# A graph network's layer 0: the node phase one block later, and reciprocal square roots on VectorE

## The chip, the cores and the metric

The kernel runs on one core of one Trainium2 chip. The metric is the device time of one execution in microseconds (us); five executions of the kernel before lie between 12327.4 and 12343.48 us, with a median of 12336.05 us. The engines are TensorE (PE in the profile, its weight loads PEld), VectorE (DVE), ScalarE (ACT), GpSimd (POOL) and SyncE (SP). DMAs are issued from the queues of SP, ACT and POOL.

## What is computed

Four graph layers run over 12500 nodes with 64 features and 212500 edges (200000 and a loop at each node); each is followed by a residual sum and a layer norm. The change touches only the first, an attention layer with 4 heads of 16 features:

```python
h = (x @ W).reshape(n, HEADS, CH)
a_src = jnp.einsum('nhc,hc->nh', h, att_src)
a_dst = jnp.einsum('nhc,hc->nh', h, att_dst)
e = jax.nn.leaky_relu(a_src[src] + a_dst[dst], NEG_SLOPE)
m = jax.ops.segment_max(e, dst, num_segments=n)
e = jnp.exp(e - m[dst])
s = jax.ops.segment_sum(e, dst, num_segments=n)
msg = h[src] * (e / (s[dst] + 1e-16))[:, :, None]
out = jax.ops.segment_sum(msg, dst, num_segments=n).reshape(n, 64) + bias
y = x + out
layer0 = (y - mean(y)) / jnp.sqrt(var(y) + 1e-5) * gamma + beta
x = _layernorm(x + layer0)
```

The next layer is a graph convolution whose edge weights are `rsqrt(deg[src]) * rsqrt(deg[dst])`; its first dense product is made at the end of layer 0's node phase. So a group of nodes needs three reciprocal square roots: one in each of two layer norms, and one of the degree.

## The kernel before

The nodes are cut into `NQ` = 128 blocks of `QB` = 98. The edges of a block lie in a tile of 128 partitions by `NJ` = 16 columns, padded. A tile of source rows, `hg`, is fetched for each block from a table in DRAM (`g0_d`), already sorted by receiving block; sums over the edges of a block are matrix products with one-hot matrices. `G` = 4 blocks are a group, of which there are 32.

Layer 0 is the stretch between about 1790 and 4025 us of the profiled execution. Its loop over blocks `d` (from L1710 on) does for each `d`:

- **Fetch** of block d+3 (L1488): one DMA from SP for `hg` (L1494) and two indirect DMAs from POOL (L1496). There are nine buffers of `hg`.
- **Place** of block d (L1585): VectorE makes the one-hot tiles `rh` (L1589), `h` (the program's `h32`, L1594, in two halves) and their product with the source scores `rv` (L1598, two halves); TensorE multiplies them into `prank` (L1603), which holds each edge's score by node and rank, and from which `largest` takes the largest score of each node. ScalarE turns `h` into `hot` (L1596), stored for the later layers. Six indirect DMAs of POOL for edge attributes (L959) follow.
- **Attend** of block d-4, which belongs to the group before (L1635): VectorE makes `ot` (L1637), TensorE multiplies it with the group's `a3` (receiver's score and maximum, in three bf16 parts) into `pd` (L1640), VectorE sums that into `ad` (L1643) and makes `z`; ScalarE takes the exponential (L1651); VectorE makes `msg` (L1652). ScalarE turns `hot` back to f32 (`o32`, L1530), and TensorE adds up `pacc` (L1532).
- After a group's fourth attend, **node0** (L1656): `xsum` out of `pacc` (L1661), two layer norms, the degree's root, a dense product (`turned4` L1390 and L1392, `dense` L1398, `tnew` L1683), and the **gather** for the next layer: `tnew` is split in three bf16 parts (L919 to L922), 42 products for each of the four blocks go to `pgat` (L931) in two halves, ScalarE copies each half to `hb` (L932) and issues the DMAs to `g_d` (L933, L934). `pgat` and `hb` have two buffers each.
- After a group's fourth place, `largest` (L1607) on VectorE and ScalarE: out of `prank` come `cnt`, `mk`, the maximum `adm`, `a3` and `pself`.

`inv_sqrt` (L1401) makes a root on ScalarE (`Sqrt`), a reciprocal and one Newton step on VectorE. ScalarE loads its function table whenever it changes between `Exp` (L1651) and `Sqrt` (L1404); those loads have the lines of the activations that need them.

SP and POOL execute in the order of the program text. On VectorE, TensorE and ScalarE a scheduler sets the order when the kernel is built, from priorities that follow the text; each engine then executes that order strictly. SP's one-hot tiles `oh` for the gather (L1511) have six buffers: the loads of a group's third and fourth one wait until the gather of the group before has used its first and second, and what stands behind them on SP (`hg`, `db` of L1706, `t0`, `x0`) waits with them.

Of the kernel before, what the change touches and what calls it, by code (L numbers as in the profile page):

```python
# [10 lines left out]
I32 = mybir.dt.int32  # L11
AF = mybir.ActivationFunctionType
OP = mybir.AluOpType
# [828 lines left out]
NQ = 128  # L842
# [7 lines left out]
G = 4  # L850
# [15 lines left out]
def tile_gnn_resnorm_d4(ctx: ExitStack, tc: tile.TileContext, a: dict, out: bass.AP):  # L866
    nc = tc.nc
    v, sca, pe, pool, sp = nc.vector, nc.scalar, nc.tensor, nc.gpsimd, nc.sync
# [453 lines left out]
    def network():  # L1322
        with ExitStack() as s0:
# [49 lines left out]
            def nt(name, w=D, bufs=2):  # L1373
                return nw.tile([QB, G, w], F32, name=name, bufs=bufs)

            def wide(t):
                return t[:QB, None, :].to_broadcast([QB, G, t.shape[-1]])

            def group(tab, g):
                return rows(tab)[:, G * g:G * g + G, :]  # L1380

            def state(tab, g, name, w=D):
                t = nt(name, w)
                sp.dma_start(t, group(tab, g))
                return t
# [15 lines left out]
            def inv_sqrt(val, shape, name):  # L1401
                sd = nw.tile(shape, F32, name=name + "_s")
                r = nw.tile(shape, F32, name=name + "_r")
                sca.activation(sd, val, AF.Sqrt)  # L1404
                v.reciprocal(r, sd)
                v.tensor_mul(sd, r, r)
                v.tensor_mul(sd, sd, val)
                v.tensor_scalar(sd, sd, -0.5, 1.5, op0=OP.mult, op1=OP.add)
                v.tensor_mul(r, r, sd)
                return r  # L1410

            def layernorm(y, dst, gamma=None, beta=None):
                s = nw.tile([QB, G], F32, name="ln_sum")
                v.tensor_reduce(out=s, in_=y, axis=AX.X, op=OP.add)
                v.tensor_scalar(s, s, -1.0 / D, None, op0=OP.mult)
                v.tensor_tensor(y, y, s[:, :, None].to_broadcast([QB, G, D]), op=OP.add)
                sq = nt("ln_sq", bufs=1)
                v.tensor_mul(sq, y, y)
                va = nw.tile([QB, G], F32, name="ln_var")
                v.tensor_reduce(out=va, in_=sq, axis=AX.X, op=OP.add)  # L1420
                v.tensor_scalar(va, va, 1.0 / D, LN_EPS, op0=OP.mult, op1=OP.add)  # L1421
                r = inv_sqrt(va, [QB, G], "ln")
                rb = r[:, :, None].to_broadcast([QB, G, D])
                if gamma is None:
                    v.tensor_tensor(dst, y, rb, op=OP.mult)
                else:
                    v.tensor_tensor(y, y, rb, op=OP.mult)
                    v.tensor_tensor(y, y, wide(gamma), op=OP.mult)
                    v.tensor_tensor(dst, y, wide(beta), op=OP.add)
# [4 lines left out]
            def heads(t):  # L1434
                return t.rearrange("p b (h c) -> p b h c", h=H)
# [52 lines left out]
            def fetch(d, w, gd, tab, parts=False):  # L1488
                if parts:
                    full = wk.tile([P, 3, NJ, w], F32, name="hg", bufs=hgbufs)  # L1490
                    hg = full[:, 0]
                else:
                    full = hg = wk.tile([P, NJ, w], F32, name="hg", bufs=hgbufs)
                sp.dma_start(hg[:, :NG, :].rearrange("p j w -> p (j w)"), gd[d].rearrange("s j w -> s (j w)"))  # L1494
                for i in range(2):
                    pool.indirect_dma_start(  # L1496
                        out=hg[:, NG + i, :], out_offset=None, in_=tab,
                        in_offset=bass.IndirectOffsetOnAxis(ap=ovr[:, d, i:i + 1], axis=0),
                        bounds_check=QB * NQ - 1, oob_is_err=False)
                return full  # L1500
# [74 lines left out]
                    gather_block(wk, pp, G * g + i, lambda k, i=i: t3[:, i, k, :], D, g_d[cur], ohs[i], hbbufs)  # L1575


            hgbufs, ohbufs, hbbufs, o32bufs = 2 * G + 1, G + 2, 2, 2
            open_phase("l0", dict(pgat=2, pacc=1, pnode=1, pd=1, prank=1))
            iotb = wk.tile([P, P], BF16, name="iotb", bufs=1)  # L1580
# [75 lines left out]
            def node0(g, xsum, acc, ps, t0, x0, ohs):  # L1656
                sl = slice(G * g, G * g + G)
                v.tensor_tensor(heads(t0[:, :, :D]), heads(t0[:, :, :D]),
                                ps[:, :, :, None].to_broadcast([QB, G, H, C]), op=OP.mult)
                v.tensor_copy(t0[:, :, D:], ps)  # L1660
                v.tensor_tensor(xsum, acc[:QB], t0, op=OP.add)  # L1661
                r = nt("r0", H)
                v.tensor_scalar(r, xsum[:, :, D:], 1e-16, None, op0=OP.add)
                v.reciprocal(r, r)
                y = nt("y")
                v.tensor_tensor(heads(y), heads(xsum[:, :, :D]), r[:, :, :, None].to_broadcast([QB, G, H, C]), op=OP.mult)
                v.tensor_tensor(y, y, wide(bias0), op=OP.add)
                v.tensor_add(y, y, x0)
                y2 = nt("y2")
                layernorm(y, y2, gamma0, beta0)  # L1670
                v.tensor_add(y2, y2, x0)
                x1 = nt("x1")
                layernorm(y2, x1)
                deg = nw.tile([QB, G], F32, name="deg4")
                v.tensor_scalar(deg, cnt[:, sl], 1.0, None, op0=OP.add)
                v.tensor_copy(dinv[:, sl], inv_sqrt(deg, [QB, G], "dg"))
                conv(g, x1, ws1[0], ohs, 0, (x_d, x1))


            def conv(g, src, w, ohs, cur, also=None):  # L1680
                ps = dense(turned4(src), w)
                t = nt("tnew")
                v.tensor_tensor(t, ps, scaled(G * g), op=OP.mult)  # L1683
                spread(g, t, ohs, cur, also)
# [22 lines left out]
                return db  # L1707

            held = []
            a3 = pself = pk = None  # L1710
            for d in range(G - 1):
                held.append([fetch(d, DH, g0_d, t0_d)])
            for d in range(NQ + G):

                g, i = divmod(d, G)
                if d + G - 1 < NQ:
                    held.append([fetch(d + G - 1, DH, g0_d, t0_d)])
                if d < NQ:
                    if i == 0:
                        pk = ps_tile([P, G // 2, 2, 256], "prank")  # L1720
                    hot = wk.tile([P, NJ, P], F8, name="hot", bufs=G + 2)
                    held[d].append(hot)
                    place(d, i, pk, held[d][0], hot)
                    pump(6)
                if G - 2 <= d < NQ + G - 2:
                    held[d - G + 2].append(load_db(d - G + 2))
                if d >= G:
                    if i == 0:
                        t0 = state(t0_d, g - 1, "t0", DH)
                        x0 = nt("x0")  # L1730
                        load_x(x0, G * (g - 1))
                        xsum = nt("xsum", DH)
                    if i == 0:
                        ps = ps_tile([P, G, DH], "pacc")
                    hg, hot, db = held[d - G]
                    add_up_whole(hot, attend(hg, db, a3[:, i]), ps[:, i, :])
                    if i == 2:
                        ohs = load_ohs(g - 1, range(2))
                    if i == G - 1:
                        ohs += load_ohs(g - 1, range(2, G))  # L1740
                        node0(g - 1, xsum, ps, pself, t0, x0, ohs)
                if d < NQ and i == G - 1:
                    a3, pself = largest(g, pk)

            open_phase("l1", dict(pgat=2, pacc=2, pnode=2))
            cur = 0
            hgbufs, ohbufs, hbbufs = AHEAD + 2, 3 * G, 4
# [5 lines left out]
            for i in range(L1N - 1):  # L1753
                run_pass(g_d[cur], tq_d[cur], None,
                         lambda g, xsum, t, ohs, i=i, cur=cur: conv(g, conv_out(g, xsum, t, i), ws1[i + 1], ohs, 1 - cur),
# [183 lines left out]
```

## Time and profile before

| | us |
|---|---|
| median of 5 runs (lowest to highest) | 12336.05 (12327.4 to 12343.48) |
| the profiled execution: its own time | 12383.26 |
| its span, first to last instruction | 12381.5 |
| busy in the span: PE, DVE, ACT, POOL | 9180.7, 8642.7, 3883.5, 6446.5 |
| mean granted clock of TensorE, as a share of full speed | 0.822 |
| first and last `xsum` (L1661) of layer 0, 32 groups | 1931.1, 4005.1 |

The profile is of one execution, which is 47 us longer than the median of the runs. A row of the timeline reads: start, duration, engine, line, operation, output<-input, shape, and in brackets how long the engine had been idle before it and what ended that. A row of the windows table reads: stretch, its length, then the busy time (and number of instructions) of PE, PEld, DVE, ACT and POOL, the granted clock of TensorE, the share of the DMA engines' time that was busy, and GB/s. Tile names in the profile lack some suffixes: `h` is `h32`, `t` is `t0` or `t3`, `a` is `a3`, `o` is `o32`, `as_r` is the remainder in the split of `a3`.

### The profile page before, as it was taken

What the parts mean: (1) busy time and instruction counts of PE and PEld (TensorE: products, weight loads), DVE (VectorE), ACT (ScalarE), POOL (GpSimd) and SP (SyncE); (2) the same over time, 40 slices, a digit from 0 to 9 for tenths busy, and PEclk for the clock granted to TensorE, in tenths of its full rate; (3) what the DMA queues carried; (4) which work ended last, traced back from release to release, by engine and by line L of the source; (5) the groups of instructions that cost most, each with busy time, mean ns of one, the idle gap of its engine ahead of it and who ended that gap; (6) DMA issues with size and microseconds to landing.
All of it is one profiled execution on the core that took longest, in us unless ns stands there. A gap on an engine that the chain in (4) does not pass through costs nothing.

```text
span 12381.5 us, 260491 instructions
## 1 busy us (share of the span) xinstructions
PE 9180.7 (74%) x102114; PEld 7601.2 (61%) x102115; DVE 8642.7 (70%) x16365; ACT 3883.5 (31%) x7061; POOL 6446.5 (52%) x4616
## 2 busy tenths in 40 slices
PE   2331657777777666666667999999899899899862
PEld 2110557777777555555556777777677677677652
DVE  6888335676766444444545888788788788799888
ACT  2330223444444122222222333333333333333300
POOL 1665555666663665665453454455355355444483
PEclk9655567888887777776667999999999999999976
DMA  2661663444443776776566777677677677677673
GB/s 91 222 228 40 213 196 110 127 134 129 126 136 103 228 228 215 235 224 214 186 189 206 242 241 235 212 242 238 212 238 241 209 239 242 205 242 257 220 211 97
DMA packets 1377992, 2414.80 MB, mean 195 GB/s; under 512 B 421097, under 2 KB 732537, under 8 KB 1376625
## 3 DMA queue, kind: packets, MB, share of 16 engines
q1 hardware_dynamic: 734770, 1565.65, 39.9%
q10 hardware_dynamic: 494495, 714.10, 16.0%
q0 software_dynamic: 147488, 118.29, 6.2%
q8 instruction: 807, 13.22, 0.4%
q14 instruction: 432, 3.54, 0.1%
HBM read 1655.94 MB, written 741.25 MB: 194 GB/s over the span
## 4 chain that ended last, share of the span: by engine, by line
PE 43%; DVE 13%; issue 10%; DMA 8%; another core or an unknown queue 4%; ACT 2%; POOL 1%; ACTq 1%; SPq 0%; POOLq 0%; DVEq 0%
PE pgat L931 10%; PE pacc L1522 9%; PE pe L1797 7%; PE p L1783 6%; PE prank L1603 3%; PE pacc L1532 3%; DVE msg L1520 2%; PE pnode L1398 2%; DMA hg<-g_d 2%; DMA g_d<-hb 1%; PE pe L1792 1%; DVE msg L1802 1%; DVE eh L1439 1%; DMA hot<-hot_d 1%
## 5 line engine op out<-in xcount | busy, mean ns | idle before, releaser
L1496 POOL DMA_INDIRECT hg<-tq_d,q_ovr x2304 | 3605.9, 1565 | 3300.0 <-DVE msg L1802 1569.5
L959 POOL DMA_INDIRECT ag<-in_edge_attr_dram,q_eid x2048 | 2485.4, 1214 | 1692.6 <-PE pattr L948 619.3
L931 PE MATMUL pgat<-t,oh 98*128 98x64 bf16 x48384 | 2073.5, 204 | 742.0 <-issue 462.8
L931 PEld LDWEIGHTS <-oh 98*128 98x128 fp8e4 x48384 | 1916.4, 105 | 1006.4 <-issue 977.2
L932 ACT COPY hb<-pgat 128x448 f32<-128x448 f32 (+1 forms) x2560 | 1309.8, 535 | 3058.0 <-PE pgat L931 1558.2
L1522 PEld LDWEIGHTS <-hot 128*128 128x128 fp8e4 x18432 | 1744.7, 105 | 745.1 <-issue 644.9
L1520 DVE TENSOR_TENSOR hg<-hg 128x1024 f32<-128x1024 f32 x1024 | 1233.7, 1219 | 779.7 <-issue 338.2
L1520 DVE TENSOR_TENSOR msg<-msg 128x1024 f32<-128x1024 f32 x1280 | 1557.7, 1217 | 3.9
L1797 PEld LDWEIGHTS pe<-we,eh 128*128 128x128 f32 x10240 | 1368.3, 192 | 226.5 <-issue 153.8
L1797 PE MATMUL pe<-we,eh 128*128 128x128 f32 x10240 | 1473.9, 280 | 4.6 <-DVE eh L1439 3.0
L1522 PE MATMUL pacc<-hg,hot 128*128 128x192 bf16 x8192 | 1106.1, 295 | 367.9 <-issue 185.6
L1438 ACT ACTIVATE eh<-p,be 128x512 f32<-128x512 f32 x1280 | 875.3, 687 | 1556.8 <-PE p L1783 1188.5
L1783 PE MATMUL p<-et,we 128*128 128x512 f32 x2560 | 1292.5, 607 | 19.5 <-ACT eh L1438 8.7
L1802 DVE TENSOR_TENSOR msg<-pe,hg 128x512 f32<-128x512 f32 x1280 | 862.3, 683 | 335.7 <-PE pe L1797 254.6
L1522 PE MATMUL pacc<-msg,hot 128*128 128x192 bf16 x10240 | 1032.0, 247 | 34.3 <-DVE msg L1520 25.4
L1603 PE MATMUL prank<-rv,h 128*128 128x161 f32 x4096 | 821.3, 362 | 239.6 <-DVE rv L1601 130.0
L1439 DVE SCALAR_TENSOR_TENSOR eh<-eh 128x512 f32<-128x512 f32 x1280 | 856.6, 682 | 89.2 <-ACT eh L1438 70.0
L1603 PEld LDWEIGHTS prank<-rv,h 128*128 128x128 f32 x4096 | 743.1, 236 | 274.4 <-DVE rv L1601 150.2
L1536 DVE TENSOR_REDUCE xsum<-pacc 98x128 f32<-98x384 f32 x576 | 318.7, 553 | 600.0 <-PE pacc L1522 425.0
L1496 POOL DMA_INDIRECT hg<-t_d,q_ovr x256 | 352.0, 1375 | 593.4 <-DVE ln_var L1421 303.4
L1178 PE MATMUL taken<-sg,hotc 128*128 128x456 bf16 x512 | 245.2, 556 | 551.6 <-issue 301.4
L1532 PE MATMUL pacc<-msg,o 128*128 128x68 f32 x4096 | 558.0, 295 | 54.1 <-issue 37.0
(327 smaller groups left out, 10516.6 us busy)
## 6 DMA issues: line engine op xcount, KB each, us to landing
hg<-g_d SPq DMA_DIRECT2D x1152, 448.0 KB
g_d<-hb ACTq DMA_DIRECT2D x1152, 416.0 KB
hot<-hot_d SPq DMA_DIRECT2D x1152, 256.0 KB
oh<-oh_d SPq DMA_DIRECT2D x1152, 171.5 KB
et<-at_d SPq DMA_DIRECT2D x640, 256.0 KB
vb<-vw_d SPq DMA_DIRECT2D x128, 912.0 KB
hg<-g_d SPq DMA_DIRECT2D x128, 476.0 KB
g_d<-hb ACTq DMA_DIRECT2D x128, 442.0 KB
```

The source lines that it names most:

```text
L931: pe.matmul(ps[:, j, :], lhsT=oh[:, 7 * hf + j, :], rhs=t3(k), start=(k == 0), stop=(k == 2))
L932: sca.copy(hb[:, 7 * hf:7 * hf + 7, :], ps)
L959: pool.indirect_dma_start(out=ag[:, j, :], out_offset=None, in_=a["edge_attr_32"], in_offset=bass.IndirectOffsetOnAxis(ap=eid[:, d, lo + j ...
L1439: v.scalar_tensor_tensor(dst, dst, 0.1, dst, op0=OP.mult, op1=OP.max)
L1496: pool.indirect_dma_start(out=hg[:, NG + i, :], out_offset=None, in_=tab, in_offset=bass.IndirectOffsetOnAxis(ap=ovr[:, d, i:i + 1], axis= ...
L1520: v.tensor_tensor(x[:, k + 1], x[:, k], top[:, k], op=OP.subtract)
L1522: pe.matmul(ps.rearrange("p (k f) -> p k f", k=3), lhsT=hot[:, j, :], rhs=top[:, :, j, :], start=(j == 0), stop=(j == NJ - 1))
L1532: pe.matmul(ps, lhsT=o32[:, j, :], rhs=x[:, hf * nj + j, :], start=(hf + j == 0), stop=(hf == 1 and j == nj - 1))
L1603: pe.matmul(pk[:, i // 2, i % 2, :RANKS * H + 1], lhsT=h32[:, j, :], rhs=rv[:, j, :], start=(hf + j == 0), stop=(hf == 1 and j == nj - 1))
L1783: pe.matmul(p1.rearrange("p q e -> p (q e)"), lhsT=w["we1"][:, j].rearrange("p t d -> p (t d)"), rhs=et, start=True, stop=True)
L1797: pe.matmul(ps[:, u:u + 2, :].rearrange("p t d -> p (t d)"), lhsT=h1[j][:, (2 * hf + q) * P:(2 * hf + q + 1) * P], rhs=w["we2"].rearrange( ...
L1802: v.tensor_tensor(msg[:, half, :], ps, hg[:, half, :], op=OP.mult)
```

## The change

Two things are changed, in layer 0 alone. First, `node0` of a group is no longer called at the end of the loop body of its last block, but in the next iteration: after `largest` of the group that is being placed, the next fetch, the next block's place and a `load_db`, and ahead of that iteration's attend. The loop runs once more for the last group. The group's `pself` is kept in `old`, since `largest` has made a new one by then. Second, `inv_sqrt` with `in_layer0` set makes no use of ScalarE: it shifts the number's bits right by one and subtracts them from a constant, on VectorE as integers, and makes three Newton steps of three VectorE instructions. Later layers keep the old form.

```diff
             def inv_sqrt(val, shape, name):
                 sd = nw.tile(shape, F32, name=name + "_s")
                 r = nw.tile(shape, F32, name=name + "_r")
+                if in_layer0:
+
+                    ri = r.bitcast(I32)
+                    v.tensor_scalar(ri, val.bitcast(I32), 1, None, op0=OP.logical_shift_right)
+                    v.tensor_scalar(ri, ri, -1, 0x5F3759DF, op0=OP.mult, op1=OP.add)
+                    for _ in range(3):
+                        v.tensor_mul(sd, r, r)
+                        v.scalar_tensor_tensor(sd, sd, -0.5, val, op0=OP.mult, op1=OP.mult)
+                        v.scalar_tensor_tensor(r, sd, 1.5, r, op0=OP.add, op1=OP.mult)
+                    return r
                 sca.activation(sd, val, AF.Sqrt)
                 v.reciprocal(r, sd)
...
-            a3 = pself = pk = None
+            a3 = pself = pk = last = None
...
-            for d in range(NQ + G):
+            for d in range(NQ + G + 1):
...
                 if G - 2 <= d < NQ + G - 2:
                     held[d - G + 2].append(load_db(d - G + 2))
-                if d >= G:
+                if last is not None:
+                    node0(*last)
+                    last = None
+                if G <= d < NQ + G:
                     if i == 0:
+                        old = pself
                         t0 = state(t0_d, g - 1, "t0", DH)
...
                     if i == G - 1:
                         ohs += load_ohs(g - 1, range(2, G))
-                        node0(g - 1, xsum, ps, pself, t0, x0, ohs)
+                        last = (g - 1, xsum, ps, old, t0, x0, ohs)
                 if d < NQ and i == G - 1:
                     a3, pself = largest(g, pk)
```

More of the change, by code (lines that the diff above doesn't have):

```diff
@@ L1575, in spread @@
                     gather_block(wk, pp, G * g + i, lambda k, i=i: t3[:, i, k, :], D, g_d[cur], ohs[i], hbbufs)
+            in_layer0 = True
             hgbufs, ohbufs, hbbufs, o32bufs = 2 * G + 1, G + 2, 2, 2
@@ L1740, in network @@
                         ohs += load_ohs(g - 1, range(2, G))
-                        node0(g - 1, xsum, ps, pself, t0, x0, ohs)
+                        last = (g - 1, xsum, ps, old, t0, x0, ohs)
                 if d < NQ and i == G - 1:
                     a3, pself = largest(g, pk)
+            in_layer0 = False
             open_phase("l1", dict(pgat=2, pacc=2, pnode=2))
```

## The prediction

> **What bounds the kernel now.** I read the windows by stage first. Layer 0 settles into rounds of one group: the chain of waits shows the same 16 products of `prank` L1603 at 2891.09, 2959.79 and 3028.07, so a round takes 68.3 us, and 1600 us hold 23.4 rounds.
>
> ```profile
> core 0: us, PE busy (x) PEld busy (x) DVE busy (x) ACT busy (x) POOL busy (x), PEclk, DMA share, GB/s
> 2200.00:3800.00 1600.00, 1244.18 (x12099) 1180.60 (x12097) 1107.98 (x2731) 694.48 (x1028) 987.51 (x767) 0.83 0.44 130
> 2959.79:2994.42 34.63, 29.14 (x242) 28.34 (x243) 28.47 (x69) 17.33 (x24) 26.48 (x19) 0.90 0.41 113
> 2994.42:3019.00 24.58, 16.18 (x223) 15.16 (x220) 10.27 (x25) 6.20 (x13) 15.05 (x14) 0.75 0.56 164
> ```
>
> Per round that is PE 53.1, DVE 47.3, ACT 29.6, POOL 42.2 us: no engine is full. The last row is the stretch of the gather: 24.6 us in which VectorE works 10.3. The waits of VectorE in the same 1600 us name the instruction:
>
> ```profile
> DVE xsum L1661 <- remote: 126.7, 11, 14.5
> DVE xsum L1661 <- PE pacc L1532: 92.8, 9, 10.9
> DVE msg L1652 <- ACT msg L1651: 65.3, 20, 5.3
> DVE xsum L1661 <- PE prank L1603: 37.2, 4, 9.7
> ```
>
> `xsum` waits 256.7 us in all, 10.9 per round, always for the group's last `pacc`. The timelines of VectorE and TensorE show what stands behind it and why it is late:
>
> ```profile
> 3005.24 1.23 DVE L1652 TENSOR_TENSOR msg<-hg,msg 128x1024 f32<-128x1024 f32 x1 [2.67 <-ACT msg L1651]
> ...
> 3009.22 0.19 DVE L920 TENSOR_TENSOR as_r<-adm,a 98x32 f32<-98x32 f32 x1 [1.17 <-ACT a L919]
> 3019.00 0.44 DVE L1661 TENSOR_TENSOR xsum<-pacc,t 98x272 f32<-98x272 f32 x1 [9.59 <-PE pacc L1532]
> 3019.48 0.19 DVE L922 TENSOR_TENSOR a<-as_r,a 98x32 bf16<-98x32 f32 x1
> ...
> 3019.67 1.48 DVE L1598 TENSOR_TENSOR rv<-rh,hg 128x1280 f32<-128x1280 bf16 x1
> 3024.12 0.56 DVE L1643 TENSOR_REDUCE ad<-pd 128x128 f32<-128x384 f32 x1 [1.32 <-PE pd L1640]
> ```
>
> ```profile
> 3009.97 1.27 PE L931 MATMUL pgat<-t,oh 98*128 98x64 bf16 x38
> 3012.26 1.78 PE L1532 MATMUL pacc<-msg,o 128*128 128x68 f32 x10 [0.46 <-issue]
> 3014.45 0.52 PE L1532 MATMUL pacc<-msg,o 128*128 128x68 f32 x3 [0.42 <-issue]
> 3015.84 0.57 PE L1532 MATMUL pacc<-msg,o 128*128 128x68 f32 x4 [0.86 <-issue]
> 3018.70 4.99 PE L1603 MATMUL prank<-rv,h 128*128 128x161 f32 x18 [0.50 <-issue]
> ```
>
> Behind `xsum` stand the last piece of `a3` (which `pd` of the next group needs) and the next block's `rv`. TensorE creeps from 3011.5 to 3018.7, waiting for "issue", while the windows give a DMA share of 1.00 and 1.05 for 3007.6 to 3014.4: the loads that SP and ScalarE send in one burst once the gather frees `oh` and `hb`. Then 18 products of `prank` take 4.99 us (277 ns each), where 16 at 2959.79 take 2.47 (154): the granted clock reads 0.50 for 3017.8 to 3021.2.
>
> **The change, part by part.** I measure a round from 0 = end of the third attend's `msg` (2989.1). Before: gather's bulk (PE x38) +7.8, fourth `msg` +16.1, `xsum` +29.9, the next group's first `ad` +35.0, end +68.3. For after I take the instruction order of the built kernel on each engine and walk one round with the durations of this trace.
>
> *ScalarE loses* four table loads and three roots per round:
>
> ```profile
> 2980.90 1.28 ACT L1404 ACT_TABLE_LOAD   x1
> 2985.10 1.28 ACT L1651 ACT_TABLE_LOAD   x1 [0.39 <-ACT hot L1596]
> ```
>
> 4 x 1.283 + 3 x 0.206 = 5.75 us of 29.6 busy. I value it at 0: ScalarE idles 38 us per round, and VectorE's waits for `msg` (65.3 / 23.4 = 2.8 per round) are at +13.5, behind the copies of `hb`, where no load stands. Its bounds are 0 and 4 x (1.283 + 0.39) = 6.7 us.
>
> The page "ScalarE: Activation LUTs" of the Trainium skill (What ACT_TABLE_LOAD costs) gives 2.66 us for a switch with its drain; 4 would be 10.6 us by it, an estimate that no term here uses; the rows show 1.283 and at most 0.39 of idle beside it. The same page (Rules for kernel authors) keeps roots on ScalarE, and "VectorE: DVE Perf Modes" (Rules for kernel authors) says that a chain of VectorE operations is made cheap only by having fewer of them; both speak against this change, and no run so far shows a root on VectorE.
>
> *VectorE gains* 11 - 5 = 6 instructions per root, 18 per round. Integer forms are not in the trace of layer 0's roots; the nearest row is L1408, a `tensor_scalar` of the same 98x4 (164 ns). Between large instructions such a row costs 0.07 us from its start to the next start (L1406 at 2963.78, L1598 at 2963.85); where one needs the other it is 0.20 (4012.36 to 4012.56). So 1.3 to 3.6 us per round; 1.5, because the order puts nearly each of them behind another instruction.
>
> *node0 moves.* SP's and POOL's lists are unchanged, and node0's own DMAs (`x_d`, `tq_d`, `g_d`) stay on ScalarE. Step by step:
>
> 1. Third `msg` to gather. TensorE now does the third `pacc` and the fourth `pd` before `pnode`: VectorE waits for `cnt` until +3.9, `ad` ends at +5.6, `x1` at +6.0, `pnode`, `xt`, dense until +8.2 (0.5 + 0.6 + 0.9), `tnew` and the splits, between `adm` (1.28), `h` and the fourth `msg` (1.2 each), until +13.3. The gather starts 5.5 us later than before. TensorE idles some 4.5 us on the way, 2.5 more than the 2.07 at 2995 and 2997.
> 2. Gather to `xsum`. VectorE has `rv`, `ot`, all of `a3`, `rh`, `h`, `rv`, `h` ahead of `xsum`: 1.4 + 0.7 + 0.2 + 0.4 + 1.15 + 1.4 + 1.15 and small ones, 7.7 us, so it comes to `xsum` at +21.0. The last `pacc` now stands ahead of the gather's fourth block: at undisturbed durations +18.9. Before, gather's bulk to last `pacc` took 21.7 us where the same sum gives 10.7, a stretch of 2.0; stretched likewise it is +24.
> 3. `xsum` to `ad`. 5.5 us of the node phase, then `ad`; its `pd` no longer waits for `a3`, but comes after the gather's end: 9.9 us after its start undisturbed (+23.2), 19.8 stretched (+33). So `ad` is between +26.5 and +33; I take +31, nearer to the stretched end, because the burst of DMAs is still triggered by the same release.
> 4. `ad` to the end of the round: before 33.3. The walk gives 30.3 at the full clock, VectorE nearly without a pause, TensorE waiting four times for 10 us together; with 0.5 clock after such gaps up to 33.3 + 1.5 = 34.8. I take 33.
>
> Round: 31 + 33 = 64.0 (26.5 + 30.3 = 56.8 to 33 + 34.8 = 67.8), 4.3 us less than 68.3. About 30 of the 32 groups have this form: 30 x 4.3 = 129 us. Cover gone: if the burst moved onto `pacc` again, `xsum` would cost what it costs now. What is late next is `rv` behind the node work, for which `prank` waits.
>
> What else moves: on SP, `hg`, `db`, `t0`, `x0` behind the blocked `oh` start at about +16 instead of +15.9 (3004.99), and the `hg` concerned is used by `rv` some 30 us later: 0. POOL waits 13.4 + 4.4 = 17.8 us per round for `msg`, so a shorter round finds it free down to about 51 (8 x 4 instructions of 1.31 with 0.30 between). The copies `o32` of the next group's first attend queue behind `hb`, at +22, and are needed at +34: 0. At the end of layer 0 nothing covers the roots: `ln_var` to product takes 4009.61 to 4013.16 and 4017.20 to 4018.47, together 4.8 us; 22 x 0.20 = 4.4 replace it: 0. Later layers have the old root and practically the old order.
>
> In this profile 12383 - 129 = 12254; the runs' median is 47 lower, so 12336 - 129 = 12207.
>
> **The rivals.**
>
> *A, slower: xsum is still late, and more work is behind it.* The gather starts 5.5 us later, and after `xsum` come 5.5 us of node work before `ad`. With 34.8 from `ad` on, the round is longer than 68.3 as soon as `xsum` starts after 68.3 - 34.8 - 5.5 = +28.0. For it: TensorE's creep, whose place in the new order I can't read. Against: the last `pacc` now precedes the fourth block. With `xsum` at +30 the round is 70.3: 30 x 2.0 = 60 us more, 12396; at the worst, +33, 12486.
>
> *B, no change: the burst sets the round.* If TensorE and the DMAs of the gather fix it, waits change names: 68.3 again, 12336. For it: DMA share of 1.0 in the burst. Against: the share is 0.44 over the round, and 10.9 us of VectorE are lost at one place.
>
> *C, more gain: the shorter gaps also lift the clock.* Undisturbed +26.5 and 31.5 give 58 to 59.5: 30 x 9.3 = 279 less, 12057. For it: clock 0.83 on average; against: the walk's four gaps.
>
> **How the numbers follow.** Forecast 0.59 (12150 to 12290), A 0.19, B 0.10, C 0.12. Likeliest: 12207. The range 12085 to 12400 leaves out C's lower half (0.06) and A's upper part (0.07), and a little of the rest. 0.2% of 12336 is 25 us, about what a measurement of this kernel can tell from no change: faster 0.59 + 0.12 = 0.71, same 0.10, slower 0.19.
>
> **What would show it.** Right: no table load and no L1404 in layer 0; the wait of `xsum` well under 10.9 per round; `a3` long before `pd`; starts of `xsum` about 64 us apart. Step 2 is wrong if `xsum` starts later than +28; step 4 if the time from the first `ad` to the third `msg` passes 35; the value 0 for ScalarE if waits for ACT `msg` vanish with the loads. The whole is wrong if rounds stay at 68.3, or if layers after 4025 us change.

## The result, and the profile after

| | before | after |
|---|---|---|
| median (lowest to highest) | 12339.29 us (12305.18 to 12406.71, 79 runs) | 12384.68 us (12316.74 to 12439.47, 42 runs) |
| ratio, 95% interval | 1 | 1.0036 (1.0028 to 1.0044) |
| span of the profiled execution | 12381.5 us | 12386.0 us |
| busy DVE, ACT | 8642.7, 3883.5 us | 8674.0, 3699.0 us |
| mean granted clock of TensorE | 0.822 | 0.818 |

The change makes the kernel 0.36% slower, some 45 us. It does what it says: the table loads and square roots of layer 0 are gone from ScalarE (6831 instructions, 230 fewer), VectorE has 576 instructions more. The changed kernel's lines from L1404 on are ten higher than before; `xsum` is L1672, `ad` L1654, `msg` L1663, `prank` L1614, `pacc` L1542. The stretches around layer 0 are practically alike: its first `h` starts at 1791.7 us before and 1789.9 after, and from its last `xsum` to the end it is 8376 and 8382 us. The profiled execution of before lay 44 us above this median, so the two spans can't be set against each other; the rounds can. From one `xsum` to the next between 2200 and 3800 us it was 67.0 us before and is 68.9 us after, and no round is like the next: some take 64 to 67 us, some 71.5, some 77 to 80.

The waits of VectorE in the changed kernel, 2200 to 3800 us (engine, what waited, for what: us in all, times, longest). "issue" stands for idle time that the profile puts down to nothing it shows, "remote" for a wait whose source the profile doesn't tell:

```profile
DVE xsum L1672 <- PE pacc L1542: 197.2, 22, 11.5
DVE ad L1654 <- PE pd L1651: 121.4, 62, 7.9
DVE a L922 <- ACT a L921: 60.9, 18, 7.6
...
DVE a L922 <- issue: 20.2, 4, 7.0
...
DVE msg L1663 <- ACT msg L1662: 8.0, 10, 1.7
```

`xsum` still waits 9 us per round, and a second stop is new: 85 us in which the last piece of `a3` (L922) waits for ScalarE's copy (L921), which stands in ScalarE's order behind a copy of `hb`. The forecast missed it. One of the long rounds on VectorE and on TensorE (timelines; the third `msg` ends at 3247.02):

```profile
3245.80 1.22 DVE L1663 TENSOR_TENSOR msg<-hg,msg 128x1024 f32<-128x1024 f32 x1
...
3269.33 0.19 DVE L922 TENSOR_TENSOR a<-as_r,a 98x32 bf16<-98x32 f32 x1 [7.00 <-issue]
...
3285.43 0.44 DVE L1672 TENSOR_TENSOR xsum<-pacc,t 98x272 f32<-98x272 f32 x1 [11.53 <-PE pacc L1542]
...
3291.16 0.56 DVE L1654 TENSOR_REDUCE ad<-pd 128x128 f32<-128x384 f32 x1 [1.54 <-PE pd L1651]
```

```profile
3262.63 1.21 PE L931 MATMUL pgat<-t,oh 98*128 98x64 bf16 x30
...
3264.97 0.36 PE L931 MATMUL pgat<-t,oh 98*128 98x64 bf16 x4 [0.43 <-issue]
3269.23 1.06 PE L931 MATMUL pgat<-t,oh 98*128 98x64 bf16 x16 [3.90 <-issue]
...
3272.91 0.23 PE L931 MATMUL pgat<-t,oh 98*128 98x64 bf16 x1 [0.50 <-issue]
3276.42 1.49 PE L931 MATMUL pgat<-t,oh 98*128 98x64 bf16 x21 [3.27 <-issue]
...
3285.18 3.96 PE L1614 MATMUL prank<-rv,h 128*128 128x161 f32 x14
...
3290.97 2.44 PE L1614 MATMUL prank<-rv,h 128*128 128x161 f32 x16
```

TensorE starts the gather at 3262.63 and creeps, as it did before, with pauses of 0.4 to 3.9 us for "issue". But the DMAs are not what it creeps under this time, and what follows is dear. The windows of the same round:

```profile
core 0: us, PE busy (x) PEld busy (x) DVE busy (x) ACT busy (x) POOL busy (x), PEclk, DMA share, GB/s
2200.00:3800.00 1600.00, 1261.58 (x11762) 1207.36 (x11761) 1099.68 (x3069) 549.26 (x837) 957.68 (x746) 0.80 0.43 126
3262.00:3276.00 14.00, 4.46 (x67) 3.29 (x66) 4.89 (x11) 0.82 (x3) 10.95 (x11) 0.61 0.10 14
3276.00:3289.00 13.00, 12.53 (x102) 12.33 (x102) 3.57 (x20) 4.65 (x8) 0.14 (x1) 0.50 0.89 270
3289.00:3319.00 30.00, 24.69 (x256) 23.68 (x255) 26.37 (x72) 12.16 (x16) 17.53 (x12) 1.00 0.44 137
```

And from the gather's bulk (the first long row of its products) to `xsum`, in a round of 65 us and in this one:

```profile
3546.70:3562.90 16.20, 11.67 (x150) 11.29 (x149) 4.93 (x12) 3.62 (x8) 11.77 (x11) 0.66 0.62 180
3262.63:3285.43 22.80, 12.79 (x149) 11.49 (x149) 4.57 (x11) 4.43 (x10) 10.64 (x10) 0.55 0.42 111
```

From 3262 to 3276 TensorE works 4.5 us of 14, with a DMA share of 0.10. From 3276 to 3289 it is busy 12.5 us of 13, and the granted clock is 0.50 the whole time: 14 products of `prank` take 3.96 us (283 ns each), where 16 take 2.44 (153) six microseconds later at the full clock. By these two rates the same work would take about half of those 12.5 us at the full clock. That is not what sets a round of 71.5 us apart from one of 65, for the low clock is in both (0.66 and 0.55): the long round has 22.8 us where the short one has 16.2, and TensorE idles 10.0 of them, not 4.5. The pauses make the difference between the two kinds of round, and the low clock comes on top in each.

### The profile page after: what moved, and what is told of

The parts are those of the page before. It is cut to its first block, busy times and chain, and to the rows that moved or that the text cites. A ratio compares the mean times of both kernels' runs of the same rounds, so it can differ in the third digit from the quotient of the medians.

```text
span 12386.0 us, 260745 instructions
## 1 busy us (share of the span) xinstructions
PE 9197.7 (74%) x102114; PEld 7632.2 (62%) x102115; DVE 8674.0 (70%) x16941; ACT 3699.0 (30%) x6831; POOL 6428.5 (52%) x4616
## 4 chain that ended last, share of the span: by engine, by line
PE 46%; DVE 19%; issue 12%; DMA 9%; another core or an unknown queue 5%; ACT 5%; POOL 2%; ACTq 1%; SPq 0%; POOLq 0%; DVEq 0%
PE pgat L931 11%; PE pacc L1532 9%; PE pe L1813 7%; PE p L1799 6%; PE pacc L1542 3%; PE prank L1614 3%; DVE msg L1530 2%; PE pnode L1398 2%; ACT sg L1175 2%; DVE top L1165 2%; DMA g_d<-hb 2%; DMA hg<-g_d 2%; ACT hb L932 2%; PE pe L1808 1%
## 5 line engine op out<-in xcount | busy, mean ns | idle before, releaser
L959 POOL DMA_INDIRECT ag<-in_edge_attr_dram,q_eid x2048 | 2531.6, 1236 | 1672.3 <-PE pattr L948 579.7
L1799 PE MATMUL p<-et,we 128*128 128x512 f32 x2560 | 1289.5, 606 | 22.3 <-DMA et<-at_d 11.4
L1614 PE MATMUL prank<-rv,h 128*128 128x161 f32 x4096 | 806.2, 358 | 154.6 <-DVE rv L1612 63.9
L1614 PEld LDWEIGHTS prank<-rv,h 128*128 128x128 f32 x4096 | 730.7, 234 | 177.3 <-DVE rv L1612 78.7
L1542 PE MATMUL pacc<-msg,o 128*128 128x68 f32 x4096 | 621.9, 320 | 80.7 <-DVE msg L1663 78.0
L1542 PEld LDWEIGHTS pacc<-msg,o 128*128 128x128 f32 x4096 | 600.7, 234 | 90.3 <-DVE msg L1663 87.3
```

The costliest lines, as they stand in the source:

```text
L959: pool.indirect_dma_start(out=ag[:, j, :], out_offset=None, in_=a["edge_attr_32"], in_offset=bass.IndirectOffsetOnAxis(ap=eid[:, d, lo + j ...
L1542: pe.matmul(ps, lhsT=o32[:, j, :], rhs=x[:, hf * nj + j, :], start=(hf + j == 0), stop=(hf == 1 and j == nj - 1))
L1614: pe.matmul(pk[:, i // 2, i % 2, :RANKS * H + 1], lhsT=h32[:, j, :], rhs=rv[:, j, :], start=(hf + j == 0), stop=(hf == 1 and j == nj - 1))
L1799: pe.matmul(p1.rearrange("p q e -> p (q e)"), lhsT=w["we1"][:, j].rearrange("p t d -> p (t d)"), rhs=et, start=True, stop=True)
```

## The experiments

Eighteen kernels ran in five sets, each beside the kernel before. The sets came out at two levels: in e1 to e4 and e9 to e12 the kernel before took 11383 and 11367 us, in the other three 12457 to 12472 us, 1% above the first measurement. In the former VectorE's and TensorE's waits in layer 0 name engines and transfers; "issue" and "remote" are hardly among them. In the latter TensorE pauses as above. The chip isn't what tells them apart: e9 to e12 and e13 to e15 ran on the same one. I call them the sets without and with pauses, and compare ratios only inside one kind. Per whole round between 2200 and 3800 us, A is the way from `xsum` to the node phase's first product (`pnode`, L1390), B the way from there to the next `xsum`; the last column is TensorE's busy time per round, its busy time in that window times the round over 1600. For the sets without pauses, whose layer 0 ends sooner, the window is 2000 to 3400 us. The row of e6 is one execution, profiled for its trace.

| with pauses | ratio (95%) | A | B | A + B | PE clock | PE busy |
|---|---|---|---|---|---|---|
| before (e6) | 1 | 34.4 | 33.8 | 68.2 | 0.82 | 53.0 |
| after, first profile | 1.0036 (1.0028 to 1.0044) | 42.9 | 26.1 | 69.0 | 0.80 | 54.4 |
| after (e5) | 1.0079 (1.0056 to 1.0102) | 47.0 | 25.4 | 72.4 | 0.78 | 56.3 |
| after (e13) | 1.0092 (1.0076 to 1.0108) | 47.1 | 24.9 | 72.0 | 0.78 | 56.3 |
| move alone (e14) | 1.0128 (1.0108 to 1.0147) | 42.4 | 31.8 | 74.2 | 0.74 | 57.3 |
| root alone (e15) | 1.0046 (1.0028 to 1.0064) | 50.3 | 20.7 | 71.0 | 0.78 | 55.1 |
| one step, old place (e18) | 1.0018 (1.0006 to 1.0030) | 38.3 | 30.1 | 68.4 | 0.81 | 53.5 |
| Ln and Exp, old place (e8) | 0.9982 (0.9968 to 0.9997) | 39.2 | 28.3 | 67.5 | 0.80 | 54.2 |
| after, more products (e16) | 0.9962 (0.9946 to 0.9978) | 39.4 | 28.1 | 67.5 | 0.85 | 57.9 |
| one step, moved (e7) | 0.9918 (0.9903 to 0.9934) | 33.7 | 30.4 | 64.1 | 0.86 | 48.5 |
| one step, moved (e17) | 0.9904 (0.9890 to 0.9919) | 33.8 | 30.9 | 64.7 | 0.85 | 49.4 |

| without pauses | ratio (95%) | round | PE clock |
|---|---|---|---|
| move alone (e1) | 1.0016 (1.0002 to 1.0029) | 57.7 | 0.83 |
| two steps, moved (e11) | 1.0034 (1.0021 to 1.0048) | 57.6 | 0.88 |
| one step, old place (e12) | 1.0034 (1.0022 to 1.0047) | 56.6 | 0.87 |
| after, `a3` split on VectorE (e3) | 1.0038 (1.0025 to 1.0051) | 58.2 | 0.86 |
| after, three `hb` (e4) | 1.0090 (1.0076 to 1.0104) | 59.2 | 0.87 |
| root alone (e2) | 1.0111 (1.0093 to 1.0129) | 60.1 | 0.85 |
| five steps, moved (e10) | 1.0181 (1.0160 to 1.0203) | 62.7 | 0.80 |
| two fillers per step (e9) | 1.0212 (1.0194 to 1.0231) | 64.2 | 0.80 |

The changed kernel's own ratio is not the same everywhere: 1.0036 at first, 1.0079 and 1.0092 in the later sets with pauses, further apart than the intervals. Why isn't known.

### The parts of the change apart: e1, e2, and with the whole e13 to e15

Move alone keeps the old `inv_sqrt`; root alone calls `node0` where it was.

```diff
-            in_layer0 = True
+            in_layer0 = False
```

```diff
-                if last is not None:
-                    node0(*last)
-                    last = None
...
-                        last = (g - 1, xsum, ps, old, t0, x0, ohs)
+                        node0(g - 1, xsum, ps, pself, t0, x0, ohs)
```

> The node phase one block later, with the old root (ScalarE's square root and its four table loads per round, VectorE's single correction). Theory M (the move alone makes the loss: last piece of a3 and xsum stop VectorE during the gather, and TensorE's clock is low for more of the time): slower than before by 0.2 to 0.7% (12360 to 12425 where before is 12339). Rival R (the 18 VectorE operations more per round are the loss; the move by itself gives what was forecast): 0.5 to 1% faster than before. With the tables back, at most 30 x 6.7 us more than the changed kernel if ScalarE's relief was worth something.

> The node phase at its old place, with the root on VectorE. Theory M: same as before within 0.2%, as the VectorE operations lie in VectorE's pauses (18 x 0.07 to 0.20 us = 1.5 to 3.6 us per round, less what the absent tables save, 0 to 6.7): between 12240 and 12430, likeliest 12330. Rival R: slower by 0.3% or more.

> The changed kernel once more, beside its two parts on one chip. Theory N (VectorE's line of work sets the round, so the root costs its added operations wherever they stand; the move is worth little): ratio to the kernel before 1.004 to 1.012, the root part alone about as much. Rival S (the parts don't add up: the built order of the whole has its own losses, as TensorE's pauses in the gather): the whole is off the sum of move alone and root alone by more than 0.4%.

> The node phase one block later with the old root, beside the whole and the other part. Where TensorE has no pauses it was 1.0016. Theory N: 0.998 to 1.003 here too. If the forecast of the move was right where TensorE pauses (4.3 us of 68 per round, and 1.5 back as no operations are added): 0.985 to 0.992.

> The root on VectorE with the node phase at its old place, beside the whole and the other part. Where TensorE has no pauses it was 1.0111. Theory N: 1.006 to 1.014 here too. Rival S: below 1.003 or above 1.017.

Without pauses the move is worth next to nothing (1.0016) and the root costs 1.1%: theory M falls there, and R holds by half, since the move gives nothing either. With pauses it is the other way round: the move alone costs 1.28% and the root 0.46%, and the whole, 1.0092, is less than the sum by 0.8%. So the parts don't add (rival S), and neither part by itself is the cause. Both parts missed what was expected of them: e14 lies above every range named for it, e15 between those of N and S. One thing that differs is the built order: in root alone `xsum` is no longer placed evenly. In most of e15, 110 and 154 of VectorE's instructions lie by turns between one `xsum` and the next (in the changed kernel 132 in nearly every round), and its starts are by turns some 61 and 84 us apart.

### VectorE's stop at a3, and hb: e3, e4

```diff
-    def split3(wk, src, dst, shape, tag):
-
+    def split3(wk, src, dst, shape, tag, copy=None):
+        copy = copy or sca.copy
         r = wk.tile(shape, F32, name=tag + "_r", bufs=1)
-        sca.copy(dst(0), src)
+        copy(dst(0), src)
         v.tensor_tensor(r, src, dst(0), op=OP.subtract)
-        sca.copy(dst(1), r)
+        copy(dst(1), r)
...
-                split3(nw, ad, lambda k: a3[:, :, k, :], [QB, G, 2 * H], "as")
+                split3(nw, ad, lambda k: a3[:, :, k, :], [QB, G, 2 * H], "as", v.tensor_copy)
```

```diff
-            hgbufs, ohbufs, hbbufs, o32bufs = 2 * G + 1, G + 2, 2, 2
+            hgbufs, ohbufs, hbbufs, o32bufs = 2 * G + 1, G + 2, 3, 2
```

> The changed kernel, with the two copies that split a3 in `largest` made by VectorE, not ScalarE. The trace of the changed kernel shows 85 us in 1600 in which VectorE's last piece of a3 waits for ScalarE's copy, which stands behind a copy of `hb`. Theory A3 (that stop delays rv, prank and then the last pacc and xsum): 2 to 3.6 us per round gone, 60 to 110 us faster than the changed kernel, so 12275 to 12325. Rival G (TensorE's gather itself sets the pace, and VectorE only waits elsewhere): the wait moves to xsum, within 25 us of the changed kernel.

> The changed kernel with three buffers of `hb`, not two, in layer 0. Theory H (the gather's copies wait for their buffer, that is for the transfer to g_d of two blocks before): the pauses of the gather shrink, 1 to 3 us per round, 30 to 90 us faster than the changed kernel. Rival G (ScalarE's copies wait for TensorE's products alone): no difference over 25 us.

Both fell into a set without pauses, where the changed kernel itself never ran; what they gain on it isn't known. In e4, whose built order has `xsum` at the same places of VectorE's as the changed kernel, L922 waits 40.9 us in 1400; in e3 the wait is gone. e3 stands 0.5% better than e4, in line with theory A3, though its order differs in more than that. They show something else: B is 13.6 and 15.6 us in them, where the forecast had 17.8. This is e4 from the gather's bulk to `xsum`, in nearly every round the same:

```profile
2768.90:2775.60 6.70, 6.63 (x149) 6.54 (x149) 4.57 (x10) 3.95 (x9) 5.47 (x5) 1.00 0.64 177
```

These are the same products (149 or 150 in the trace) as in the two rows of the changed kernel above, in 6.7 us, not 16.2 or 22.8: TensorE never pauses, and its clock is 1.00. The DMA share is 0.64, in the round of 65 us above it was 0.62, so a DMA share of this size doesn't by itself stretch the way. The third `hb` is not the reason either: e1 and e3, with two, have no pauses for "issue".

### The number of Newton steps: e5 to e7, e10 to e12, e17, e18

```diff
-                    for _ in range(3):
+                    for _ in range(1):
```

(`range(5)` in e10, `range(2)` in e11; e12 and e18 have one step and the old place of `node0`; e5 is the changed kernel, e6 the one before.)

> The changed kernel itself, unaltered, to have its trace and its ratio where the first four experiments ran: there the kernel before took 11383 us, not 12336, and no `issue` wait of TensorE was in the traces. Theory O (the loss comes from the order in which VectorE works and from its added operations, whatever the pace of TensorE): ratio to the kernel before 1.003 to 1.010. Rival K (the loss comes from TensorE's creep and its clock, which were seen only in the slower profiles): ratio 0.990 to 1.000, as forecast, once the creep is gone.

> The kernel before, with blank lines so that its line numbers are those of the changed one: only for its trace beside the others. Theory O: VectorE's waits for `xsum` are as long as in the changed kernel or shorter. Rival K: they are 5 us per round longer than in the changed kernel.

> The changed kernel with one Newton step per root, not three (layer 0's roots are then off by up to 0.2%): as many VectorE operations as before the change, no table loads. Theory O with the price of the added operations at 0.07 to 0.20 us each: 18 fewer per round, 31 rounds, 40 to 110 us (0.35 to 1.0%) less than the changed kernel. Rival P (the place of the node phase and the order set the loss, the operations hide in pauses): within 25 us of the changed kernel.

> The changed kernel with five Newton steps per root, not three: 18 more VectorE operations per round, of which 12 stand in the chain from xsum to the gather. Theory C: the two roots take 9 to 11 us more (as the step from five to eleven operations did: 13.3 against 22), the round 4 to 9 us more than with three, ratio 1.018 to 1.030. Rival N: 1.3 to 3.6 us per round, ratio 1.010 to 1.017.

> The changed kernel with two Newton steps per root (exact to about 5e-6). Theory C: between one step (ratio 0.992, roots 13.3 us together) and three (1.004 to 1.008, 21.5 to 23 us): roots 16 to 19 us, ratio 0.996 to 1.003. Rival N: 9 x 0.07 to 0.20 us per round less than three steps, ratio 1.000 to 1.006.

> One Newton step per root, the node phase at its old place (layer 0's roots off by up to 0.2%). It tells what the move is worth where the chain is short. If the move shortens the way from the gather to xsum by what the traces show (31 to 34 us before, 25 to 30 in the moved kernels), the ratio is 0.996 to 1.004, worse than the 0.992 of one step with the move. If the move is worth nothing, 0.988 to 0.994.

> One Newton step with the move, beside the same without it. Where TensorE pauses: 0.9918 again. Where it doesn't: if the move is worth what it was with the old root (1.0016, nothing), 1.000 to 1.005, as one step without it (1.0034); if it is worth 4 us per round there too, 0.985 to 0.995.

> One Newton step at the old place, beside the same with the move. Where TensorE doesn't pause: 1.0034 again. Where it does: if the move is worth its 4 us per round as long as the chain is short, 1.000 to 1.006; if the gain of one step came from the root alone, 0.989 to 0.995.

With pauses, one step is 1.6 to 1.9% faster than three (0.9918 and 0.9904 against 1.0079 and 1.0092), about 200 to 230 us or 6.5 to 7.5 us per round for 18 operations, about twice the most that their price of 0.07 to 0.20 us allows (3.6 us). Without pauses, three steps more (e11 to e10, 27 operations) cost 1.47%, 167 us or 5.4 us per round, 0.20 us each: the upper end of the price. e5 met a set with pauses again, so K's case was not tested; of the kernels that ran where TensorE doesn't pause, none is faster than before. e6 fits neither theory: VectorE waits 249.9 us for `xsum` in it and 188.1 in e5, some 2 us per round longer, where O had it no longer and K 5 us longer. e10 lies at the lower end of theory C's range and just above N's, e11 within N's and just above C's. The pair e17 and e18 gives the move's worth with a short root: 1.1%. With the old root the same move costs 1.28% (e14).

Why a root's length matters is seen on VectorE. This is one root of the changed kernel (timeline; L1410 to L1412 are a Newton step, L1437 uses the result):

```profile
3221.85 0.16 DVE L1407 TENSOR_SCALAR ln_r<-ln_var 98x4 int32<-98x4 int32 x1
...
3223.63 0.15 DVE L1412 SCALAR_TENSOR_TENSOR ln_r<-ln_s,ln_r 98x4 f32<-98x4 f32 x1
3223.71 1.22 DVE L1605 TENSOR_TENSOR h<-q_dl,iotb 128x1024 f32<-128x1024 bf16 x1
3224.84 0.15 DVE L1410 TENSOR_TENSOR ln_s<-ln_r 98x4 f32<-98x4 f32 x1
3224.91 1.22 DVE L1663 TENSOR_TENSOR msg<-hg,msg 128x1024 f32<-128x1024 f32 x1
3226.05 0.15 DVE L1411 SCALAR_TENSOR_TENSOR ln_s<-ln_s,ln_var 98x4 f32<-98x4 f32 x1
...
3229.74 0.42 DVE L1437 TENSOR_TENSOR y<-y,ln_r 98x256 f32<-98x256 f32 x1
```

Most of the chain's operations have another, often a large one, behind them, so eleven operations of some 0.15 us take 7.9 us from first to result. From `ln_var` to the product, both layer norms together, the mean is 11.8 us before, 13.2 with one step, 21.5 after (first profile) and 22.9 (e5, e13). In e4, which doesn't pause, it is 21.8.

### Is it the chain? e9

```diff
+                    pad = [nw.tile(shape, F32, name=name + f"_p{q}") for q in range(2)]
+                    def fill():
+                        for q in pad:
+                            v.tensor_mul(q, val, val)
                     v.tensor_scalar(ri, val.bitcast(I32), 1, None, op0=OP.logical_shift_right)
+                    fill()
```

(and so after each of the eleven operations)

> The changed kernel with two small products on scratch tiles written after each operation of a layer 0 root, so that VectorE has something short to do while a result of the chain gets ready: 66 more VectorE operations per round, and in the built order no large operation stands inside the second layer norm's root and almost none inside the first's. Theory C (the root is a chain of eleven dependent operations on the way from xsum to the gather, and each step waits for the large operation that the order puts behind it; in the changed kernel the two roots of a round take 21.5 to 23 us together, before 12): the two roots take 5 to 9 us together, the round loses 3 us or more against the changed kernel, ratio to the kernel before 0.985 to 1.000. Rival N (the number of VectorE operations costs, wherever they stand): 66 x 0.07 to 0.20 = 4.6 to 13 us per round more, ratio 1.02 to 1.04.

```profile
2518.12 0.17 DVE L1420 SCALAR_TENSOR_TENSOR ln_r<-ln_s,ln_r 98x4 f32<-98x4 f32 x1
2518.19 0.24 DVE L1410 TENSOR_TENSOR ln_p<-ln_var 98x4 f32<-98x4 f32 x2
2518.34 0.17 DVE L1416 TENSOR_TENSOR ln_s<-ln_r 98x4 f32<-98x4 f32 x1
2518.41 0.24 DVE L1410 TENSOR_TENSOR ln_p<-ln_var 98x4 f32<-98x4 f32 x2
```

The timeline shows the chain as intended, a step each 0.22 us; the two roots fall to 7.4 us. And the kernel is 2.1% slower. So theory C falls where TensorE doesn't pause: the chain's length alone is not what costs. What is not done between its steps is done after it, since VectorE works in one order. 84 operations more than before cost 241 us (0.0212 of 11367), over 31 rounds 0.09 us each: rival N's price.

### Is it the clock? e16

In the table with pauses, the round (A + B) less TensorE's busy time is 14.6 to 16.9 us in nine of the ten rows without added products and 13.3 in e8, while the busy time for the same products goes from 48 to 57 us as the clock goes from 0.86 to 0.74. To tell cause from company, e16 gives TensorE more to do:

```diff
+                    if hf == 0:
+                        for j in range(4):
+                            pe.matmul(pk[:, i // 2, i % 2, :P], lhsT=h32[:, j, :], rhs=iota, start=True, stop=True)
                     for j in range(nj):
                         pe.matmul(pk[:, i // 2, i % 2, :RANKS * H + 1], lhsT=h32[:, j, :], rhs=rv[:, j, :],
...
                     sca.copy(o32, hot[:, hf * nj:hf * nj + nj, :])
+                    if hf == 0:
+                        for j in range(4):
+                            pe.matmul(ps, lhsT=o32[:, j, :], rhs=iota[:, :ps.shape[-1]], start=True, stop=True)
```

> The changed kernel with 32 added products per round on TensorE (four of 128 columns ahead of each block's prank, four of 68 ahead of each block's pacc, overwritten by the real ones; 154 and 140 ns each at the full clock, so about 4.7 us per round), ready while VectorE still makes the operand that the real ones wait for; VectorE's order is nearly the same. Theory K (TensorE's granted clock carries the loss, and falls for its pauses): the share of the half clock falls by 0.05 or more, and the round is no longer, ratio 0.990 to 1.010. Rival W (TensorE's own work is what the round waits for, or the clock doesn't follow its business): 2.4 to 4.7 us per round more than the changed kernel, ratio 1.010 to 1.025 where TensorE doesn't pause, 1.015 to 1.03 where it does.

Windows 2200 to 3800 us of the changed kernel (e13) and, in the second fence, of e16; then TensorE's waits in e16:

```profile
2200.00:3800.00 1600.00, 1251.07 (x11185) 1203.74 (x11185) 1044.98 (x2916) 522.38 (x795) 898.96 (x714) 0.78 0.42 120
```

```profile
2200.00:3800.00 1600.00, 1371.43 (x13525) 1317.67 (x13524) 1117.36 (x3122) 563.31 (x855) 977.52 (x759) 0.85 0.44 129
```

```profile
PE pgat L931 <- issue: 105.2, 133, 5.3
...
PE prank L1620 <- DVE rv L1615: 12.9, 22, 0.8
...
PE pacc L1545 <- DVE msg L1669: 2.5, 5, 0.6
```

The same two waits in e13, and in the kernel before (first profile):

```profile
PE pacc L1542 <- DVE msg L1663: 72.9, 42, 4.0
...
PE prank L1614 <- DVE rv L1612: 28.0, 32, 2.7
```

```profile
PE prank L1603 <- DVE rv L1601: 100.7, 73, 2.7
...
PE pacc L1532 <- DVE msg L1652: 1.4, 5, 0.3
```

With 32 products more per round the kernel is faster than the changed one by 1.2 to 1.3% (0.9962 against 1.0079 and 1.0092) and faster than before. The gather pauses no less (105.2 us), and from its bulk to `xsum` it takes 16.0 us as in e13; B is even longer, 28.1 us and not 24.9. What is gone are the short waits for `msg` (57.4 us in the first profile, 72.9 in e13) and `rv` (44.8 and 28.0), and with them the low clock: 0.96 in stretch A, where e13 has 0.84, and A is 39.4 us instead of 47.1. So rival W falls: where TensorE pauses, filling its waits for VectorE lifts the clock, and the kernel gains more than the added products cost.

Against the kernel before, the clock carries the loss in the sum: from e6 to e13 the round grows by 3.8 us and TensorE's busy time for the same products by 3.3. But that the change lost it by more waits of this kind isn't shown. The two waits come to 102 us before (at a clock of 0.83), 102 in the first profile after (0.80) and 101 in e13 (0.78), and with one step moved (e17) TensorE waits 143.5 us for `rv` ahead of `pd` alone, at 0.85. So theory K holds in its first half, that the clock carries the loss; which pauses of the new order lower the clock stays open.

### Ln and Exp on ScalarE: e8

```diff
+                    sca.activation(sd, val, AF.Ln)
+                    sca.activation(r, sd, AF.Exp, scale=-0.5)
+                    v.tensor_mul(sd, r, r)
+                    v.scalar_tensor_tensor(sd, sd, -0.5, val, op0=OP.mult, op1=OP.mult)
+                    v.scalar_tensor_tensor(r, sd, 1.5, r, op0=OP.add, op1=OP.mult)
+                    return r
```

> The node phase at its old place, the root as exp(-0.5 ln x) on ScalarE with one Newton step on VectorE: three VectorE operations per root (before: five, changed kernel: eleven) and, if Ln and Exp lie in one table, no table loads in layer 0. Theory O: 31 x 6 x (0.07 to 0.20) = 13 to 37 us less for VectorE and up to 6.7 us per round for ScalarE, so faster than before by 0.1 to 1%. If Ln and Exp need two tables, slower than before by 0.3% or more. Rival P: within 0.2% of before.

Ln and Exp were not given one table: 141 loads stand in 1600 us, 5.9 per round against 4 before. It is 0.18% faster than before all the same, so two more loads per round on ScalarE cost less than two VectorE operations fewer per root give, or than the new order gives; which, wasn't separated.

## Why the prediction was wrong, step by step

Means over the whole rounds, in the prediction's own terms (us from the end of the third `msg`; the first profiles of before and after, 24 and 23 rounds; e13, 21; e4, 22):

| | before | forecast | after | e13 | e4, no pauses |
|---|---|---|---|---|---|
| the gather's bulk | +7.3 | +13.3 | +16.0 | +17.6 | +14.8 |
| `xsum` | +30.4 | +24 | +33.1 | +33.6 | +21.5 |
| first `ad` | +34.7 | +31 | +38.6 | +38.9 | +29.0 |
| end of the round | +66.9 | +64.0 | +68.9 | +72.2 | +59.2 |

- **What bounds the kernel.** The reading named the wait and the creep, and noted the clock (0.50 for 3017.8 to 3021.2), but made no term of it. The place of `xsum`'s wait was taken for what the round loses; one step with the move has that wait in full (268 us in 1600, e7) and rounds of 64 us. And 68.3 us for a round was read from two rounds; the mean is 67.0, so even 64.0 would have been a gain of 3 us, not 4.3.
- **ScalarE's relief at 0.** With pauses, move alone, which has the tables and fewer VectorE operations, is 0.36% slower than the whole (1.0128 and 1.0092), some 45 us or 1.5 us per round: inside the bounds of 0 and 6.7, but from kernels whose orders differ.
- **VectorE's 18 operations at 1.5 us.** As busy time right: 46.4 us per round before, 47.4 after. As time of the round too low: 5.4 us for 27 where TensorE doesn't pause, 6.5 to 7.5 us for 18 where it does. There the clock is lower with them as well (0.78 against 0.85); what links the two wasn't shown.
- **Step 1**, gather at +13.3: it starts 2.7 us later (first profile), 4.3 in e13.
- **Step 2 is the step that failed.** "Stretched likewise it is +24"; `xsum` starts at +33.1. From the gather's bulk to `xsum` 10.7 us were forecast; 17.0 are measured in the first profile and 16.0 in e13. That is 6.3 us too many, the largest miss of the four. Of the 17.0 us TensorE is busy 11.6, at a clock of 0.67, and idle 5.5, of which 4.3 for "issue". In e4 the same products take 6.7 us, with neither. The delay was carried over as a factor: 21.7 over 10.7 before, so 2.0 times the 5.6 us of the walk (which gives +24.5, where +24 was written). As an addition, 11.0 us on the same 5.6, it would have put `xsum` at +29.9, beyond the +28.0 from which rival A holds; the measured addition is 11.4 us. Nor did the delay belong to the burst of DMAs: in the round above the pauses came with a DMA share of 0.10, and e4 has 0.64 without a pause. The order of the instructions was read right: undisturbed, step 2 has VectorE at `xsum` at +21.0, and e4 has it at +21.5. That `a3` comes "ahead of" `xsum` without waiting was wrong as well: 85 us of stops at L922.
- **Step 3**, `ad` some 7 us after `xsum`: 5.5 us.
- **Step 4**, 33 us from `ad`: 30.3 in the first profile, better than forecast; 33.4 in e13, as forecast.
- **The sum.** 64.0 was forecast, 68.9 came (72.2 in e13): 2.7 and 6.3 us too many in steps 1 and 2, 1.5 and 2.7 too few in steps 3 and 4. That one step with the move has 64 us is no confirmation: it gets there by A = 33.8 and B = 30.9 (e17), the forecast by 46.2 and 17.8.
- **The rivals.** A's condition, `xsum` later than +28, is what happened. That its 12396 was near is luck in part: with `xsum` at +33.1 and its own 5.5 and 34.8 us behind it the round would take 73.4 us. C, that the gaps of the new order decide the clock, had the right agent and the wrong sign.
- **What would show it.** No table loads and unchanged later layers were right, and so was `a3` "long before `pd`": it is ready 15 to 21 us ahead, where it was 0.1 to 4.2 before. `xsum`'s wait "well under 10.9" was not (9). The sign against step 2, `xsum` later than +28, came true.

One Newton step with the move is faster than both kernels where TensorE pauses (0.9904 and 0.9918). It leaves layer 0's roots off by up to 0.2%, and it wasn't run where TensorE doesn't pause. Not tried: the changed kernel without pauses, `a3` split on VectorE with them, and the kernel before with the added products of e16.

## What to carry to other kernels

Where TensorE is busy three quarters of a round and its clock reads about 0.8, price an edit by what it does to TensorE's small waits, not only by the busy time it adds or the one long wait it removes: here 32 useless products per round were worth 1.2%. Before a delay is carried over to a new order, ask whether it scales with the work under it or is added to it; here it was an addition of some 11 us to 10.7 us of work and to 5.6 alike. A tiny operation on VectorE cost 0.09 us (e9) to 0.20 us (e10 against e11) here, and about twice that where TensorE paused. Where a scheduler sets the order, measure the parts of a change together, since they don't add (1.0128 and 1.0046 against 1.0092).

## What the hardware did that was not expected

- The clock stayed at 0.50 for 13 us in which TensorE was busy 12.53 us. The page "TensorE: Matmul & The Clock Gate" of the Trainium skill (Part 1: The HAM clock gate) lets the full clock return after one busy window of about 3.4 us; the measurement decides. It warns of idle gaps of more than about 3 us (Why this matters for your kernels); the waits for `msg` that e16 filled were mostly shorter (72.9 us in 42 of them, the longest 4.0), and filling them raised the clock all the same.
- The kernel before took 11367 and 11383 us in two sets of runs and 12457 to 12472 in three. TensorE's pauses for "issue", in small groups some 0.7 us apart (3270.77, 3271.49, 3272.20 and 3272.91 in the trace of after), are in the traces of the slower sets. What makes them was not found: they come with a DMA share of 0.10 as with 1.0, and one chip had a set with them and a set without.
